# Ternary feed-forward stages of an eight-batch macaron block: most groups' activations transposed by DMA instead of TensorE

## The chip, the cores and the metric

The kernel runs on one core of one Trainium2 chip. The metric is the device time of the whole program in microseconds (us). The profile calls the engines PE (TensorE matrix multiply), PEld (TensorE weight load, which overlaps PE), DVE (VectorE), ACT (ScalarE), POOL (GpSimd) and SP (SyncE, which here issues DMAs).

## The reference

`x` holds 8 x 1024 tokens of width 256. Six sublayers are applied one after the other, each with a residual add and a layernorm in front. They are an FP4-quantized feed-forward, a decaying linear attention, the FP4 feed-forward again, a ternary feed-forward, a memory attention, and the ternary feed-forward again. The ternary feed-forward, the only sublayer that the change touches, is this:

```python
def _L1_ffn_ref(x, W1, b1, W2, b2):
    def _ternary(w):
        scale = jnp.maximum(jnp.mean(jnp.abs(w)), 1e-08)
        w_t = jnp.clip(jnp.round(w / scale), -1.0, 1.0)
        return w + jax.lax.stop_gradient(w_t - w)
    h = jnp.einsum('bsd,fd->bsf', x, _ternary(W1)) + b1
    h = jax.nn.gelu(h, approximate=False)
    return jnp.einsum('bsf,df->bsd', h, _ternary(W2)) + b2
...
x = x + 0.5 * _L1_ffn_ref(_layernorm(x, axis=-1), ...)
```

Its width is 256 in, 1024 hidden, 256 out. The weights are -1, 0 or 1.

## The kernel before

The 8192 tokens stay in SBUF for the whole program as 16 tiles `X[g]` (NG = 16), each [128 partitions, G = 4, D = 256] in float32, that is 512 tokens (TG). A tile is called a group. `ffn_ternary` is called twice, for the fourth sublayer (`ffn_ternary(False, "memory")`) and the sixth (`ffn_ternary(True)`). Below, "the first" and "the second ternary stage" mean these two.

In a ternary stage a group goes through four steps.

- **norm(g)** (L1155): four DVE instructions write the normalized group, tokens in the partitions, into `xn`. `xn_pool` has one buffer.
- **norm_turn(g)** (L1174 to L1179): the matmuls need the feature in the partitions, so PE transposes 2 x 4 blocks of 128x128 against an identity into two PSUM tiles `pt` of one bank each (pool `ps_t`, two buffers). The float32 value is then carried as a sum of two float32r parts: ACT copies `pt` to `xh` (the high part), and DVE writes `xl = pt - xh` (the rest).
- **hidden(g)** (L1193 to L1204): for each of NF = 8 slices of the hidden width, four matmuls of 512 columns (`xh` and `xl`, two halves of the features) fill a PSUM tile `ph` (pool `ps_h`, four buffers). ACT applies Gelu with the bias and writes `hf` in SBUF (L1201; pool `f1_t`, four buffers), copies it to the high part `hh` (L1202), and DVE writes `hl = hf - hh` (L1204).
- **down(g)** (L1220, L1228): for each of the four token tiles, 16 matmuls of 256 columns fill `po` (two banks), and DVE adds half of it to `X[g]`. In the second stage SP then writes the group to HBM.

The loop runs `norm_turn(g)`, `hidden(g-1)` and `down(g-2)` in its round g. Between the slices of `hidden` the entries of a list `between` are called, one for each slice: `norm(g+1)`, `ln.advance(g)` (the layernorm statistics of later groups, DVE, L235 and L236, and the small instructions that turn them into factors, L248 to L264) and, in the last rounds of the first stage, the statistics of the next stage. The last four slices add the output bias to `X` on DVE (`biased`, L1165).

`PLANS["ternary"]` says in what blocks of groups the statistics are taken, (2, 2, 4, 4, 4), and by which round each group's have to be there, `g - 1`. `statistics` spreads the work over the rounds between.

Within an engine the instructions run in the order in which the tile scheduler put them. In these stages the order is not written out by hand (`loose`): the scheduler takes them by priority, roughly the program's order, and puts ready work into gaps. All PSUM (8 banks) is in use: 2 for `pt`, 4 for `ph`, 2 for `po`.

The same program already transposes by DMA in the FP4 stages: SP issues `dma_start_transpose` of a [128, 768] bf16 tile `gd` into `gt` (L912) and of a [128, 512] one into `gtx` (L1084).

Of the kernel before, what the change touches and what calls it, by code (L numbers as in the profile page):

```python
# [9 lines left out]
F32 = mybir.dt.float32  # L10
F32R = mybir.dt.float32r
BF16 = mybir.dt.bfloat16
I32 = mybir.dt.int32
AF = mybir.ActivationFunctionType
ALU = mybir.AluOpType
AX = mybir.AxisListType
PSUM = bass.MemoryType.PSUM

P = 128
D = 256  # L20
# [3 lines left out]
G = 4  # L24
TG = G * P
# [14 lines left out]
def macaron_kernel(  # L40
# [25 lines left out]
    nc = tc.nc  # L66
    NB, S, _ = x.shape
    NG = NB * S // TG
# [21 lines left out]
    xn_pool = ctx.enter_context(tc.tile_pool(name="xn_pool", bufs=1))  # L90
# [39 lines left out]
    for g in range(NG):  # L130
        xg = xpool.tile([P, G, D], F32, name=f"x_{g}")
        X.append(xg)
        if g == 0:
# [4 lines left out]
                out=A0.lng[:, H : H + 2], in_=gamma_rep.rearrange("(m p) -> p m", p=P)  # L138
# [11 lines left out]
    b1c = w_l1.tile([P, NF], F32, name="b1c")  # L150
# [11 lines left out]
    for m in range(NM):  # L162
        nc.sync.dma_start(
            out=mem_d[:, :, m, :],
            in_=memories[m].rearrange("h d e -> (h d) e").rearrange("(c p) e -> p c e", p=P),
        )
        nc.sync.dma_start(
            out=nrm_d[:, :, m],
# [99 lines left out]
    def statistics(sizes, dues):  # L268
# [81 lines left out]
        "fp4": ((3, 1, 2, 4, 4, 2), [0 if g < 3 else G * (g - 2) + 2 for g in range(NG)]),  # L350

        "decay": ((2, 2, 4, 4, 4), [max(0, G * g - 5) for g in range(NG)]),
        "ternary": ((2, 2, 4, 4, 4), [max(0, g - 1) for g in range(NG)]),

        "memory": (
            (GB + 3, 3, 4, NG), [max(0, G * (g - GB) - 4) for g in range(NG)]
# [4 lines left out]
    def begin(kind, left):  # L361

        if kind not in begun:
            ln = statistics(*PLANS[kind])
            begun[kind] = [ln, list(ln.first)]
        ln, shares = begun[kind]
        for _ in range(-(-len(shares) // left)):
            shares.pop(0)()
        if left == 1:
            xn = xn_pool.tile([P, G, D], F32, tag="xn", name="xn")  # L370
            ln.normalize(xn, 0)
            begun[kind] = (ln, xn)
# [26 lines left out]
    def transpose_group(src, dst, psum, tag, both_act=False, pin=lambda ins: ins):  # L399

        for k in range(2):
            pt = psum.tile([P, TG], F32, tag=tag, name="pt")
            for j in range(G):
                pin(
                    nc.tensor.transpose(
                        pt[:, j * P : (j + 1) * P], src[:, j, k * P : (k + 1) * P], ident
                    )
                )
            if k == 0 or both_act:
                nc.scalar.copy(dst[:, k, :], pt)  # L410
            else:
                pin(nc.vector.tensor_copy(dst[:, k, :], pt))

    def fp4_first(xn, mg, pool):

# [722 lines left out]
    def ffn_ternary(last, after=None):  # L1138
        with ExitStack() as st:
            lnp = st.enter_context(tc.tile_pool(name="f1_ln", bufs=2))  # L1140
            hp = st.enter_context(tc.tile_pool(name="f1_h", bufs=2))
            tp = st.enter_context(tc.tile_pool(name="f1_t", bufs=4))
            ps_t = st.enter_context(tc.tile_pool(name="f1_pt", bufs=2, space=PSUM))
            ps_h = st.enter_context(tc.tile_pool(name="f1_ph", bufs=4, space=PSUM))
            ps_o = st.enter_context(tc.tile_pool(name="f1_po", bufs=2, space=PSUM))
            xns, xts, hs = {}, {}, {}
            ln, xns[0] = begun.pop("ternary")
            loose.append("ternary")

            def norm(g):  # L1150
                xn = xn_pool.tile([P, G, D], F32, tag="xn", name="xn")
                for j in range(G):
                    n = G * g + j
                    pin(
                        nc.vector.tensor_scalar(  # L1155
                            xn[:, j, :], X[g][:, j, :], ln.mv[:, n, 0:1], ln.lr[:, n : n + 1],
                            ALU.subtract, ALU.mult,
                        )
                    )
                xns[g] = xn  # L1160

            def biased(j, g):

# [3 lines left out]
            def norm_turn(g):  # L1167
                xn = xns.pop(g)
                xh = lnp.tile([P, 2, TG], F32R, tag="xh", name="xh")
                xl = lnp.tile([P, 2, TG], F32R, tag="xl", name="xl")  # L1170
                for k in range(2):
                    pt = ps_t.tile([P, TG], F32, tag="pt", name="pt")
                    for j in range(G):
                        nc.tensor.transpose(  # L1174
                            pt[:, j * P : (j + 1) * P], xn[:, j, k * P : (k + 1) * P], ident
                        )
                    nc.scalar.copy(xh[:, k, :], pt)
                    pin(
                        nc.vector.tensor_tensor(  # L1179
                            xl[:, k, :], pt, xh[:, k, :].bitcast(F32), ALU.subtract  # L1180
                        )
                    )
                xts[g] = (xh, xl)

            def hidden(g, between):
                xh, xl = xts.pop(g)
                hh = hp.tile([P, NF, TG], F32R, tag="hh", name="hh")
                hl = hp.tile([P, NF, TG], F32R, tag="hl", name="hl")
                for f in range(NF):
                    ph = ps_h.tile([P, TG], F32, tag="ph", name="ph")  # L1190
                    for k in range(2):
                        for xt in (xh, xl):
                            nc.tensor.matmul(  # L1193
                                ph,
                                lhsT=w1[:, k, f * P : (f + 1) * P],
                                rhs=xt[:, k, :],
                                start=(k == 0 and xt is xh),
                                stop=(k == 1 and xt is xl),
                            )
                    hf = tp.tile([P, TG], F32, tag="hf", name="hf")  # L1200
                    nc.scalar.activation(hf, ph, AF.Gelu, bias=b1c[:, f : f + 1])  # L1201
                    nc.scalar.copy(hh[:, f, :], hf)  # L1202
                    pin(
                        nc.vector.tensor_tensor(  # L1204
                            hl[:, f, :], hf, hh[:, f, :].bitcast(F32), ALU.subtract
                        )
                    )
                    if f < len(between):
                        between[f]()
                    elif f >= NF - G:  # L1210
                        biased(f - NF + G, g)
                hs[g] = (hh, hl)
# [24 lines left out]
            for g in range(NG + 2):  # L1237
                between = []
                if g < NG:
                    norm_turn(g)  # L1240
                    if g + 1 < NG:
                        between.append(lambda: norm(g + 1))
                    between.append(lambda: ln.advance(g))
                    if after and g >= NG - 6:
                        between.append(lambda: begin(after, NG - g))
                if 0 <= g - 1 < NG:
                    hidden(g - 1, between)
                else:
                    for do in between:
                        do()  # L1250
                if 0 <= g - 2 < NG:
                    down(g - 2)
# [853 lines left out]
```

## Time and profile before

| | |
|---|---|
| three runs | 2587.45, 2589.17 (median), 2592.93 us |
| the profiled execution | 2594.43 us, of which the span from first to last instruction is 2592.7 us |
| mean granted TensorE clock | 0.993 |
| first ternary stage, from the first to the last of its instructions on the chain | about 1487 to 1749 us |
| second ternary stage | about 2319 to 2590 us |
| DMA, mean over the span | 51 GB/s; 138048 of 199897 packets are under 512 bytes |

A row of the groups of instructions reads: line, engine, operation, output<-inputs, shape, count | busy us in all, mean ns of one | idle time of the engine just before them and what ended most of it. A row of a stretch reads: start:end, its length, then busy us and number of instructions for PE, PEld, DVE, ACT and POOL, then granted PE clock, share of the DMA engines' time, and GB/s. A row of the chain of waits reads: start us, us, what. That chain is followed back from the last instruction, at each step to what released it.

Busy times of overlapping matmuls add up to more than their pitch: the 32 matmuls of 512 columns of a group have a mean of about 400 ns each and take 7.47 us on the chain.

### The profile page before, as it was taken

Reading aid. Unit: us, or ns where it says so; the run is one execution under the profiler, and the core shown is the slowest. Engines: PE = TensorE matmul, PEld = TensorE weight load, DVE = VectorE, ACT = ScalarE, POOL = GpSimd, SP = SyncE. Lnnn points to the kernel's source line nnn. Section 1 sums busy time; section 2 is a strip of 40 time slices with the busy share of each in tenths; the row PEclk is TensorE's granted clock in tenths of the full one; section 3 lists DMA queues with packets and bytes.
Section 4 is the critical chain, followed back from the end, with each engine's and each line's share of the span. In section 5 each row is a group of like instructions: output and inputs, shape, how many; then the busy total and the mean of one; then the engine's idle time right before and its main releaser. Section 6 shows DMA issues by size and latency. Waiting matters only on the chain.

```text
span 2592.7 us, 52415 instructions
## 1 busy us (share of the span) xinstructions
PE 2506.9 (97%) x20426; PEld 1868.6 (72%) x20426; DVE 2087.8 (81%) x4808; ACT 1235.1 (48%) x2785; POOL 900.9 (35%) x895
## 2 busy tenths in 40 slices
PE   4899999999999999999999999999999999999999
PEld 2577777766666666777777689995677776778998
DVE  7898888758878778988888599647888888879864
ACT  5344444334333333444444276656555555437664
POOL 4565555521101003555555300004555555530000
PEclk9899999999999999999999999999999999999999
DMA  7455556500000002556555300000000000000001
GB/s 218 87 117 115 113 118 116 107 23 18 10 22 14 2 2 48 114 116 115 117 116 113 66 1 1 1 1 1 2 2 2 2 2 2 2 2 26 33 33 41
DMA packets 199897, 132.40 MB, mean 51 GB/s; under 512 B 138048, under 2 KB 174944, under 8 KB 199648
## 3 DMA queue, kind: packets, MB, share of 16 engines
q1 hardware_dynamic: 198704, 127.85, 22.8%
q8 instruction: 161, 2.64, 0.4%
q0 software_dynamic: 240, 0.54, 0.1%
q14 instruction: 88, 0.72, 0.1%
q10 hardware_dynamic: 704, 0.66, 0.1%
HBM read 80.77 MB, written 16.52 MB: 38 GB/s over the span
## 4 chain that ended last, share of the span: by engine, by line
PE 84%; DVE 11%; ACT 2%; issue 1%; DMA 1%; POOL 1%; SPq 0%; DVEq 0%; POOLq 0%; ACTq 0%
PE po L960 11%; PE pu L861 10%; PE pg L861 10%; PE po L1220 9%; PE ph L1193 9%; PE sc L1263 5%; PE py L1347 5%; PE pq L1361 4%; PE pkv L1361 4%; PE po L1361 4%; PE pk L1361 4%; PE py L1329 2%; PE pmo L1786 2%; DVE at L1272 1%; DVE qp L804 1%
## 5 line engine op out<-in xcount | busy, mean ns | idle before, releaser
L960 PE MATMUL po<-wd,ht 128*128 128x256 f32 x1536 | 358.1, 383 | 0.6 <-DVE x L969 0.5
L861 PE MATMUL pu<-wgu,xt 128*128 128x352 f32 x1024 | 349.6, 464 | 8.3 <-DVE h L876 7.9
L861 PE MATMUL pg<-wgu,xt 128*128 128x352 f32 x1024 | 348.8, 463 | 4.4 <-ACT sg L871 4.1
L960 PEld LDWEIGHTS po<-wd,ht 128*128 128x128 f32 x1536 | 294.6, 193 | 62.4 <-issue 2.2
L871 ACT ACTIVATE sg<-pg 128x352 f32<-128x352 f32 x256 | 118.1, 461 | 451.5 <-PE pg L861 422.6
L817 POOL TENSOR_TENSOR h<-h,q_rs 128x704 f32<-128x704 f32 (+1 forms) x128 | 176.2, 1376 | 413.1 <-DVE q_rs L811 413.1
L861 PEld LDWEIGHTS pu<-wgu,xt 128*128 128x128 f32 x1024 | 186.5, 193 | 112.3 <-issue 19.6
L861 PEld LDWEIGHTS pg<-wgu,xt 128*128 128x128 f32 x1024 | 195.0, 191 | 97.8 <-ACT sg L871 9.2
L1220 PE MATMUL po<-w,hl 128*128 128x256 f32 x1024 | 243.7, 280 | 1.4 <-DVE hl L1204 1.2
L1220 PE MATMUL po<-w,hh 128*128 128x256 f32 x1024 | 243.3, 280 | 0.0
L1902 POOL TENSOR_TENSOR mo<-mo 128x256 f32<-128x256 f32 x192 | 164.2, 855 | 196.6 <-DVE mo L1799 188.1
L927 POOL TENSOR_TENSOR ht<-gt,ht 128x768 f32<-128x768 bf16 x124 | 205.7, 1659 | 0.0
L1193 PE MATMUL ph<-xh,w 128*128 128x512 f32 x512 | 204.4, 401 | 1.4 <-ACT hf L1201 0.6
L1193 PE MATMUL ph<-xl,w 128*128 128x512 f32 x512 | 201.8, 395 | 0.0
L1204 DVE TENSOR_TENSOR hl<-hf,hh 128x512 fp32r<-128x512 f32 x256 | 168.3, 684 | 39.4 <-ACT hh L1202 35.9
L1220 PEld LDWEIGHTS po<-w,hl 128*128 128x128 f32 x1024 | 192.1, 188 | 4.5 <-DVE hl L1204 2.5
L1220 PEld LDWEIGHTS po<-w,hh 128*128 128x128 f32 x1024 | 192.1, 188 | 2.6 <-DVE x L1228 0.3
L1201 ACT ACTIVATE hf<-ph,b1c 128x512 f32<-128x512 f32 x256 | 168.0, 695 | 18.5 <-PE ph L1193 16.1
L1272 DVE TENSOR_TENSOR at<-sc,dec 128x512 f32<-128x512 f32 x256 | 158.6, 682 | 11.8 <-PE sc L1263 11.8
L886 DVE SCALAR_TENSOR_TENSOR h<-qp,h 128x704 f32<-128x704 f32 x124 | 110.2, 889 | 69.1 <-ACT qp L821 68.9
L1272 DVE TENSOR_TENSOR at<-sc,tri 128x512 f32<-128x512 f32 x256 | 164.9, 679 | 0.4 <-PE sc L1263 0.4
L1202 ACT CAST hh<-hf 128x512 fp32r<-128x512 f32 x256 | 149.2, 628 | 17.0 <-PE po L1220 15.2
(276 smaller groups left out, 5303.0 us busy)
## 6 DMA issues: line engine op xcount, KB each, us to landing
ht<-sd SPq DMA_DIRECT2D x124, 384.0 KB
xt<-sd SPq DMA_DIRECT2D x56, 256.0 KB
sd<-sct SPq DMA_DIRECT2D x124, 64.0 KB
x<-in_x SPq DMA_DIRECT2D x15, 512.0 KB
out<-x SPq DMA_DIRECT2D x15, 512.0 KB
t_raw<-in_w_t SPq DMA_DIRECT2D x16, 256.0 KB
gt<-gd SPq DMA_TRANSPOSE x124
gtx<-xn SPq DMA_TRANSPOSE x56
```

Source lines behind the costliest of these rows:

```text
L817: pin(mul.tensor_tensor(vb, vb, rs[:, :, None].to_broadcast([P, nb, 16]), ALU.mult))
L861: nc.tensor.matmul(ps, lhsT=xts[g][:, 2 * j + k, :], rhs=wgu[:, k, (2 * q + of_up) * NHALF : (2 * q + of_up + 1) * NHALF], start=(k == 0), ...
L927: nc.gpsimd.tensor_tensor(wide.rearrange("p c t -> p (c t)"), grid.rearrange("p c t -> p (c t)"), wide.rearrange("p c t -> p (c t)"), ALU. ...
L960: nc.tensor.matmul(po, lhsT=ht[:kn, c, :], rhs=wd[:kn, c, :], start=(c == 0), stop=(c == NC - 1),)
L1193: nc.tensor.matmul(ph, lhsT=w1[:, k, f * P : (f + 1) * P], rhs=xt[:, k, :], start=(k == 0 and xt is xh), stop=(k == 1 and xt is xl),)
L1201: nc.scalar.activation(hf, ph, AF.Gelu, bias=b1c[:, f : f + 1])
L1202: nc.scalar.copy(hh[:, f, :], hf)
L1204: nc.vector.tensor_tensor(hl[:, f, :], hf, hh[:, f, :].bitcast(F32), ALU.subtract)
L1220: nc.tensor.matmul(po, lhsT=ht[:, f, j * P : (j + 1) * P], rhs=w2[:, f, :], start=(f == 0 and ht is hh), stop=(f == NF - 1 and ht is hl),)
L1272: nc.vector.tensor_tensor(at, sc.rearrange("p m (e t) -> p (m e) t", e=2), weight, ALU.mult)
L1361: nc.tensor.matmul(dst, lhsT=lhsT, rhs=rhs, start=n == 0, stop=n == len(parts) - 1)
L1902: summed = nc.gpsimd.tensor_tensor(mo[:, :, :, 0, :], mo[:, :, :, 0, :], mo[:, :, :, m, :], ALU.add)
```

## The change

Groups 0 to 2 of each ternary stage are transposed by PE as before. For groups 3 to 15 (`by_dma`):

- `norm` writes `xn` into a pool of its own (one buffer), two rounds ahead instead of one. `planes_turned` lets POOL take the float32 words apart into two planes of 16-bit halves (two copies of 1024 elements a partition) and SP transposes both planes, [128, 2048] of 16 bits, in one DMA (two buffers of `turned`).
- `norm_turn` lets POOL join the halves again (`planes_joined`: four copies of 512 elements a partition) into `xf` (one buffer). A function `split` does the rest, and is put at the end of `between`: one ACT copy of 1024 elements to `xh`, and `xl = xf - xh` on POOL instead of DVE.

For all groups, Gelu writes over its input `ph` in PSUM instead of `hf` in SBUF. `hh` and `hl` are then read from `ph`, whose bank is free only after `hl`. `ps_t` and the pool of `hf` are gone. `ps_h` has six buffers instead of four and gives the `pt` of groups 0 to 2 as well. The plan of the statistics has due times one round earlier and smaller first blocks.

```diff
-        "ternary": ((2, 2, 4, 4, 4), [max(0, g - 1) for g in range(NG)]),
+        "ternary": (
+            (2, 2, 2, 2, 4, 4), [0 if g < 2 else 1 if g == 2 else g - 2 for g in range(NG)]
+        ),
...
+    def planes_turned(xn, pool):
+        words = xn.rearrange("p t d -> p (t d)").bitcast(U16).rearrange("p (n b) -> p n b", b=2)
+        apart = pool.tile([P, 2, G * D], U16, tag="apart", name="apart")
+        for b in range(2):
+            nc.gpsimd.tensor_copy(apart[:, b, :], words[:, :, b])
+        turned = pool.tile([P, 2, 2 * G, P], U16, tag="turned", name="turned")
+        nc.sync.dma_start_transpose(
+            out=turned.rearrange("p b n t -> p (b n) t"),
+            in_=apart.rearrange("p b n -> p (b n)"),
+        )
+        return turned
+
+    def planes_joined(turned, dst):
+        words = dst.rearrange("p k t -> p (k t)").bitcast(U16)
+        words = words.rearrange("p (k j t b) -> p b k j t", k=2, j=G, b=2)
+        for b in range(2):
+            for k in range(2):
+                nc.gpsimd.tensor_copy(
+                    words[:, b, k],
+                    turned[:, b].rearrange("p (j k) t -> p k j t", k=2)[:, k],
+                )
...
-            tp = st.enter_context(tc.tile_pool(name="f1_t", bufs=4))
-            ps_t = st.enter_context(tc.tile_pool(name="f1_pt", bufs=2, space=PSUM))
-            ps_h = st.enter_context(tc.tile_pool(name="f1_ph", bufs=4, space=PSUM))
+            gp = st.enter_context(tc.tile_pool(name="f1_g", bufs=2))
+            ps_h = st.enter_context(tc.tile_pool(name="f1_ph", bufs=6, space=PSUM))
...
+            by_dma = lambda g: g > 2
...
-                xn = xn_pool.tile([P, G, D], F32, tag="xn", name="xn")
+                if by_dma(g):
+                    xn = gp.tile([P, G, D], F32, tag="xn", name="xn", bufs=1)
+                else:
+                    xn = xn_pool.tile([P, G, D], F32, tag="xn", name="xn")
...
-                xns[g] = xn
+                xns[g] = planes_turned(xn, gp) if by_dma(g) else xn
...
+                xts[g] = (xh, xl)
+                if by_dma(g):
+                    xf = gp.tile([P, 2, TG], F32, tag="xf", name="xf", bufs=1)
+                    planes_joined(xn, xf)
+
+                    def split():
+                        nc.scalar.copy(xh, xf)
+                        nc.gpsimd.tensor_tensor(xl, xf, xh.bitcast(F32), ALU.subtract)
+
+                    return split
                 for k in range(2):
-                    pt = ps_t.tile([P, TG], F32, tag="pt", name="pt")
+                    pt = ps_h.tile([P, TG], F32, tag="ph", name="pt")
...
-                    hf = tp.tile([P, TG], F32, tag="hf", name="hf")
-                    nc.scalar.activation(hf, ph, AF.Gelu, bias=b1c[:, f : f + 1])
-                    nc.scalar.copy(hh[:, f, :], hf)
+                    nc.scalar.activation(ph, ph, AF.Gelu, bias=b1c[:, f : f + 1])
+                    nc.scalar.copy(hh[:, f, :], ph)
                     pin(
                         nc.vector.tensor_tensor(
-                            hl[:, f, :], hf, hh[:, f, :].bitcast(F32), ALU.subtract
+                            hl[:, f, :], ph, hh[:, f, :].bitcast(F32), ALU.subtract
                         )
                     )
...
-                    norm_turn(g)
-                    if g + 1 < NG:
-                        between.append(lambda: norm(g + 1))
+                    split = norm_turn(g)
+                    for m in (g + 1, g + 2):
+                        if m < NG and by_dma(m) == (m == g + 2):
+                            between.append(lambda m=m: norm(m))
                     between.append(lambda: ln.advance(g))
                     if after and g >= NG - 6:
                         between.append(lambda: begin(after, NG - g))
+                    if split:
+                        between.append(split)
```

More of the change, by code (lines that the diff above doesn't have):

```diff
@@ L13 @@
 I32 = mybir.dt.int32
+U16 = mybir.dt.uint16
 AF = mybir.ActivationFunctionType
@@ L1182, in norm_turn @@
                     )
-                xts[g] = (xh, xl)
             def hidden(g, between):
```

## The prediction, made before the changed kernel was run

> **What bounds the kernel now.** I read the page's busy times first, then the chain of waits in the ternary stages, then those stages in stretches.
>
> ```profile
> PE 2506.9 (97%) x20426; PEld 1868.6 (72%) x20426; DVE 2087.8 (81%) x4808; ACT 1235.1 (48%) x2785; POOL 900.9 (35%) x895
> ```
>
> PE is busy almost throughout. The chain of the first ternary stage shows whether a group's period is PE work alone:
>
> ```profile
> 1646.55 0.87 PE pt L1174 x8
> 1647.42 7.47 PE ph L1193 x32
> 1654.89 7.54 PE po L1220 x64
> 1662.43 0.87 PE pt L1174 x8
> ```
>
> It is. A group takes 1662.43 - 1646.55 = 15.88 us: 0.87 for the eight transposes, 7.47 for `hidden`, 7.54 for `down`, and no wait. The 13 groups from 1515 us on look so, as do 13 in the second stage (from 2356 us). Earlier rounds differ, see below. Next, what the other engines have left (columns: PE, PEld, DVE, ACT, POOL, clock, DMA share, GB/s):
>
> ```profile
> 1500.00:1516.00 16.00, 14.41 (x82) 11.92 (x82) 16.00 (x57) 13.02 (x24) 0.00 (x0) 1.00 0.00 2
> 1568.00:1584.00 16.00, 16.00 (x107) 14.47 (x106) 15.94 (x56) 10.35 (x20) 0.00 (x0) 1.00 0.01 2
> 1648.00:1664.00 16.00, 16.00 (x106) 14.52 (x105) 10.84 (x23) 10.33 (x19) 0.00 (x0) 1.00 0.00 1
> ```
>
> POOL and DMA are idle here. DVE is full until about 1600 us because statistics are taken ahead of need, then busy 10.84 of 16. Only at 1500 to 1516 does PE fall short while DVE is full: there the chain runs over DVE (1491.5 to 1506.7 us).
>
> **What goes.** Per DMA group: eight transposes on PE, two copies on ACT, two subtractions on DVE.
>
> ```profile
> L1201 ACT ACTIVATE hf<-ph,b1c 128x512 f32<-128x512 f32 x256 | 168.0, 695 | 18.5 <-PE ph L1193 16.1
> ...
> L1202 ACT CAST hh<-hf 128x512 fp32r<-128x512 f32 x256 | 149.2, 628 | 17.0 <-PE po L1220 15.2
> ...
> L1179 DVE TENSOR_TENSOR xl<-pt,xh 128x512 fp32r<-128x512 f32 x64 | 41.2, 680 | 1.5 <-ACT xh L1177 1.5
> ```
>
> The mean of a transpose (L1174) is 278 ns, but they overlap: the chain pays 0.87 us for eight, not 2.2. With PE as the bound, 13 groups x 2 stages x 0.87 = **-22.6 us**. DVE loses 2 x 0.68 = 1.36 us a group, which is off the path. A group then takes 7.47 + 7.54 = 15.01 us of PE, and everything else must fit into that.
>
> **What comes, engine by engine.**
>
> POOL, per group: two copies of 1024, four of 512, one subtraction of 1024. No row shows a 16-bit strided copy. The rows nearest, and the far ones:
>
> ```profile
> L1902 POOL TENSOR_TENSOR mo<-mo 128x256 f32<-128x256 f32 x192 | 164.2, 855 | 196.6 <-DVE mo L1799 188.1
> ...
> L1680 POOL TENSOR_SCALAR rt<-rt 96x128 f32<-96x128 f32 x64 | 41.5, 648 | 20.6 <-ACT rt L1674 17.6
> ...
> L1486 POOL TENSOR_TENSOR x<-x,ob 128x1024 f32<-128x1024 f32 x16 | 38.2, 2385 | 341.2 <-ACT xn L317 303.8 <-DVE w L721 22.1 <-DVE t_raw L717 15.3
> ...
> L386 POOL TENSOR_TENSOR xn<-xn,q_rs 128x1024 f32<-128x1024 f32 x2 | 3.9, 1930 | 5.7 <-DVE q_rs L385 5.7
> ...
> L475 POOL CAST df<-ii 128x128 f32<-128x128 int32 x1 | 0.3, 289 | 0.0
> ...
> L484 POOL CAST sf<-ii 128x1 f32<-128x1 int32 x1 | 0.2, 187 | 0.0
> ```
>
> The two CAST rows, one input as in the new copies, give (289 - 187)/127 = 0.80 ns an element over 187 ns: 1.01 us for 1024, 0.60 for 512. With the subtraction at 2.39 (L1486) that is 2.02 + 2.40 + 2.39 = 6.8 us a group. Upper ends: L1902 at 855/256 = 3.34 ns gives 4096 x 3.34 + 2.39 = 16.1 us; L1680 at 648/128 = 5.06 gives 23.1. I take 6.8, since the CAST rows are the same kind of instruction: POOL is under half full, cost nothing. The cover ends at 15.01 us, or (15.01 - 2.39)/4096 = 3.1 ns an element.
>
> DMA, per group: 16 blocks of 128x128. The chain and a stretch in the FP4 stage show 4 blocks (`gtx`) among other transfers, and 6 (`gt`) nearly alone:
>
> ```profile
> 1435.73 4.81 DMA gtx<-xn
> ```
>
> ```profile
> 1426.00:1427.40 1.40, 1.40 (x8) 1.17 (x7) 1.33 (x4) 0.00 (x0) 0.01 (x1) 1.00 1.02 141
> ```
>
> That stretch holds the packets of one `gt`: 196 KB in 1.4 us. So 512 KB takes 3.7 us plus about 1.2 to issue; scaling 4.81 by four instead gives 19.2. I take 5 to 6. SP queues nothing in the first stage but the transposes; in the second, the writes of `out`, ready a round's end later, so neither waits long for the other. Latency: `norm(g+2)` early in round g, joined by round g+2, over 20 us to spare.
>
> ACT: the `xh` copy of 1024 is estimated at 1.05 us (L1202's slope over 512, doubled, less one start), instead of 2 x 0.59. Gelu into PSUM: ACT copies into PSUM of 512 take 621 ns (`mgx`, L821) against 624 within SBUF (L1202), and `hh` from PSUM is like `xh` from `pt`, 587. So 8 x (0.69 + 0.59) + 1.05 = 11.3 of 15.01, nothing.
>
> The new waits: `xh` on ACT waits for POOL's joins; behind it are Gelu and so PE's `ph`. POOL can join group g as soon as `xl` of g-1 is done, a round early, so the wait is empty at 6.8 us. `norm(g+2)` on DVE waits for POOL to have taken group g+1 apart; behind it are the `hl`. That was a round ago.
>
> PSUM: slices in flight between PE and `hl` fall from 8 (four `ph`, four `hf`) to 6. In steady rounds, slice 7 starts 6.5 us into `hidden` and needs `hl` of slice 1, which before was done at 4.8: 1.7 us spare.
>
> **Where I charge something:** the first rounds. At 1503.5 us PE has done ten slices and DVE three `hl`: seven in flight. Six buffers, two of which hold `pt` of group 2, cut that by one to three slices of 0.93 us. Also `norm(3)`, 4 x 0.41 = 1.6 us of DVE, comes a round earlier into rounds where DVE is full. Bounds: 0 (the scheduler puts `hl` first) to 1.6 + 2.8 = 4.4 us a stage, in the far case with nothing regained. I take **3 us a stage, +6**. The extra block of statistics (12 small DVE instructions, pitch about 0.08 us) is in this.
>
> **Sum:** -22.6 + 6 = -16.6 us. The profiled execution, 2594.43 (span 2592.7), would become 2577.8. It ran 5.3 us above the median; the terms are differences of PE time, so the median becomes 2589.17 - 16.6 = **2572.6 us**. Without the charge it is 2566.6; with all of it 2575.4.
>
> DVE beside POOL: L1956 (DVE, two SBUF inputs, in a stage where POOL works) ranges from 241 to 816 ns, up to 0.575 us more. Here the four bias adds a group (L1165) have two SBUF inputs; the new `hl` reads PSUM for one. 4 x 0.575 = 2.3 us fits DVE's spare time in steady rounds (10.84 - 1.36 = 9.5 of 15.01): nothing.
>
> **Rules that speak against it.** The page "VectorE: DVE Perf Modes" of the Trainium skill, section The three transpose paths, gives 1309 ns for a 128x128 block by DMA and 390 on TensorE, and sends 128x128 transposes to TensorE where PSUM will do. By it, 16 blocks would be an estimated 20.9 us a group, over the period, and the change (20.9 - 15.88) x 26 = 131 us slower; the stretch above, six blocks in 1.4 us, contradicts reading it as a rate. The page "GPSIMD Engine Reference" of the same skill, section 4.1 Engine selection, advises against POOL for two-input elementwise work, about half VectorE's speed; the one such instruction a group, 2.39 us by L1486, still fits under the period.
>
> **Rivals.**
> 1. *POOL becomes the bound (slower, 14%).* Mechanism: strided 16-bit copies run at the far rows' rates; `xl` then arrives late for `hidden`. It loses time against before from (15.88 - 2.39)/4096 = 3.3 ns an element on. At L1902's 3.34: (16.1 - 15.88) x 26 = +6, with the start's +6 near 2600; at L1680's 5.06: (23.1 - 15.88) x 26 = +188, 2777. For: no row of a 16-bit strided copy. Against: 0.80 ns for one-input rows.
> 2. *DMA becomes the bound (slower, 3%):* 19.2 us a group, (19.2 - 15.88) x 26 = +86, 2675. Against: the stretch above.
> 3. *Only part is gained (14%):* in the DVE-full rounds up to 1600 us (and to 2425 in the second stage) late `hl` hold `ph`, and PE stops for about 1 us a group in six groups a stage: +12, 2584.6. Against: the 1.7 us spare.
> 4. *Nothing changes (5%):* PE waits elsewhere for what it saves, 2589. Against: a chain of PE alone.
>
> The forecast has 64%, between 2563 (no charge, and DVE's relief helping the start) and 2579. 0.2%, about what a measurement here can tell from no change, is 5.2 us: below 2584 is faster. Rival 3 straddles that, two thirds above faster. Faster: 0.64 + 0.10 = 0.74. Same: 0.04 + 0.05 = 0.09. Slower: 0.17. The range, 2562 to 2596, takes in forecast, rivals 3 and 4, and leaves out rivals 1 and 2.
>
> **What would show it.** Right: in the chain `ph` follows `po` with no `pt` from group 3 on, period 15.0; POOL 6 to 8 us a group; `xh` idle on POOL near zero. Wrong: PE idle before `ph` with a releaser POOL (`xl`), DMA (`turned`) or DVE `hl`; copies of 1024 above 3.2 us; a start longer than 5 us over before's.

## The result, and the profile after

The changed kernel takes 2616.09 us (median of 4 runs, 2614.40 to 2617.88), against 2588.31 for the kernel before (4 runs, 2585.21 to 2592.93). The ratio is 1.0106, 95% interval 1.0088 to 1.0123: slower by 27.8 us, where 16.6 us of gain were forecast, and outside the range. The profiled executions are nearer to each other (spans 2614.4 and 2592.7, +21.7), since that of before (2594.43 us) ran above all four of its timed runs.

Line numbers are now those of the changed kernel: `ph` L1232, `po` L1258, `hl` L1242, `xn` L1185, bias add L1195, `x<-po` L1266, taking apart L422, joining L436, `xl` L1208. First the page's busy times:

```profile
PE 2495.6 (95%) x20218; PEld 1850.1 (71%) x20218; DVE 2100.8 (80%) x4780; ACT 1222.8 (47%) x2759; POOL 1096.3 (42%) x1077
```

PE has 208 instructions fewer (26 groups x 8 transposes) and was busy 11.3 us less, over a span that is 21.7 longer: the time went into waiting. Where, the chain of waits says. This is a piece of the first ternary stage, early and late (start us, us, what):

```profile
1579.51 1.20 DVE hl L1242 x2
1580.80 0.65 DVE x L1195 x2
1581.44 1.20 DVE hl L1242 x2
1582.64 3.05 DVE xn L1185 x3
1585.69 1.20 DVE hl L1242 x2
...
1651.57 7.54 PE po L1258 x64
1659.10 7.47 PE ph L1232 x32
1666.57 7.54 PE po L1258 x64
1674.11 7.47 PE ph L1232 x32
```

From 1650 us on it is what was forecast: no `pt`, and 15.01 us a group (7.54 + 7.47). Ahead of that, where the chain of before was PE from 1515 us on, it now runs over DVE. One piece stands out: three `xn` in 3.05 us, which at 0.41 each would be 1.2. The same two places in the stretches (start:end, length, busy us and instructions of PE, PEld, DVE, ACT, POOL, granted clock, DMA share, GB/s):

```profile
1575.00:1590.00 15.00, 11.66 (x71) 9.87 (x70) 15.00 (x38) 8.12 (x14) 7.04 (x7) 0.96 0.19 36
1665.00:1680.00 15.00, 15.00 (x97) 13.54 (x96) 6.76 (x12) 9.75 (x18) 5.21 (x5) 1.00 0.18 35
```

In the first stretch DVE is "busy" for all 15 us with 38 instructions, and PE idles 3.3 us. In the second DVE needs 6.76 and PE never waits. POOL, ACT and the DMA engines have time to spare in both. So DVE is the bound of the early rounds, though the change took work off it. The groups of DVE instructions between 1500 and 1650 us, shapes kept apart, show which became dearer:

```profile
L1242 DVE TENSOR_TENSOR hl<-ph,hh 128x512 fp32r<-128x512 f32 x71 | 46.8, 677 | 0.3 <-ACT hh L1240 0.3
L1195 DVE TENSOR_TENSOR x<-x,b2h 128x256 f32<-128x256 f32 x62 | 30.9, 510 | 0.0
L1185 DVE TENSOR_SCALAR xn<-x,ln_mv,ln_r 128x256 f32<-128x256 f32 x56 | 29.1, 569 | 1.1 <-POOL apart L422 1.1
```

and the same in the kernel before, between 1500 and 1600 us:

```profile
L1204 DVE TENSOR_TENSOR hl<-hf,hh 128x512 fp32r<-128x512 f32 x55 | 36.2, 678 | 0.3
...
L1165 DVE TENSOR_TENSOR x<-x,b2h 128x256 f32<-128x256 f32 x34 | 13.5, 413 | 0.0
L1155 DVE TENSOR_SCALAR xn<-x,ln_mv,ln_r 128x256 f32<-128x256 f32 x29 | 10.4, 406 | 0.1
```

`hl` costs what it did; the bias adds went from 413 to 510 ns in the mean and `xn` from 406 to 569. A mean hides the form of such a rise. The query by source line gives minimum, median and maximum: 380, 405 and 2501 ns for `xn`. The typical one is unchanged and a few take over 2 us, so I looked at those in the timeline, with POOL's at the same time:

```profile
1532.44 2.37 DVE L265 SCALAR_TENSOR_TENSOR ln_r<-ln_h,ln_r 128x8 f32<-128x8 f32 x1
...
1549.50 2.82 DVE L1185 TENSOR_SCALAR xn<-x,ln_mv,ln_r 128x256 f32<-128x256 f32 x2
```

```profile
1532.40 2.39 POOL L1208 TENSOR_TENSOR xl<-xf,xh 128x1024 fp32r<-128x1024 f32 x1 [5.36 <-ACT xh L1207]
...
1549.68 2.48 POOL L1208 TENSOR_TENSOR xl<-xf,xh 128x1024 fp32r<-128x1024 f32 x1 [8.65 <-ACT xh L1207]
```

The first is an instruction of eight elements a partition, 0.16 us elsewhere. It began 0.04 us after a POOL instruction of 2.39 us and ended at 1534.81, 0.02 us after it. The two `xn` end at 1552.32, POOL's at 1552.16. The DVE instructions of the two stages that took over 0.1 us longer than their shape elsewhere, 70 in all, each end within 0.3 us of the end of a POOL instruction. They are of two kinds: those with two tensors from SBUF (bias adds, the terms `ln_h` and `ln_r`), and `tensor_scalar` (`xn`, `ln_va`). The profile counts the wait as busy time, so no view of waits names POOL for it. It names the next in line:

```profile
PEld po L1258 <- DVE x L1266: 10.4, 9, 2.3
PEld ph L1232 <- DVE hl L1242: 10.0, 13, 1.7
PE po L1258 <- DVE x L1266: 8.2, 7, 2.1
```

(us in total, times, longest.) `hl` and `x<-po` are not slow; they stand behind a DVE instruction that waits for POOL.

The table has what I worked out from each trace. A stage reaches from the first `ph` matmul to the last `po` matmul. "DVE waiting" is the time of DVE instructions beyond what the same shape takes with POOL idle, summed over a stage, first and second; a stretch in which two wait at once (e6, e7) counts once. Stages and waiting are those of the one profiled execution of each kernel.

| kernel | median us | ratio to before, 95% interval | stages, us | DVE waiting, us | longest |
|---|---|---|---|---|---|
| before | 2588 to 2592 | | 256.8, 257.0 | 0, 0 | |
| after | 2616.09 | 1.0106, 1.0088 to 1.0123 | 265.3, 268.8 | 23.6, 23.3 | 2.2 |
| e1 no turning by DMA | 2596.24 | 1.0025, 1.0016 to 1.0035 | 257.2, 257.2 | 0, 0.1 | |
| e2 order kept | 2619.11 | 1.0109, 1.0094 to 1.0124 | 270.4, 267.8 | 22.4, 20.8 | 2.3 |
| e3 Gelu in SBUF | 2655.60 | 1.0248, 1.0233 to 1.0263 | 287.9, 289.1 | 44.3, 42.7 | 2.1 |
| e4 short POOL pieces | 2605.43 | 1.0054, 1.0038 to 1.0071 | 259.5, 264.0 | 10.9, 12.1 | 0.6 |
| e5 short, order kept | 2599.46 | 1.0034, 1.0020 to 1.0047 | 259.0, 257.8 | 10.0, 7.9 | 0.6 |
| e6 DVE relieved | 2631.01 | 1.0152, 1.0135 to 1.0169 | 273.2, 272.4 | 24.9, 21.5 | 2.7 |
| e7 relieved, short | 2642.16 | 1.0207, 1.0167 to 1.0247 | 286.6, 290.4 | 35.7, 36.5 | 10.3 |
| e8 turning left out | 2576.64 | 0.9942, 0.9928 to 0.9957 | 245.3, 247.1 | 0, 0 | |
| e9 groups 8-15, short | 2599.29 | 1.0031, 1.0019 to 1.0043 | 258.8, 259.4 | 5.8, 5.9 | 0.6 |
| e10 groups 8-15, long | 2603.34 | 1.0049, 1.0034 to 1.0064 | 260.9, 259.6 | 12.2, 10.4 | 2.2 |
| e11 as e1, old plan | 2596.74 | 1.0019, 1.0010 to 1.0029 | 258.5, 258.5 | 0, 0 | |
| e12 groups 6-15, short, order kept | 2589.06 | 0.9992, 0.9982 to 1.0001 | 254.3, 253.4 | 5.4, 5.7 | 0.6 |
| e13 as e12, order from hidden(3) | 2584.65 | 0.9978, 0.9969 to 0.9988 | 251.4, 250.8 | 5.4, 5.6 | 0.6 |
| e14 as e13, long pieces | 2619.62 | 1.0115, 1.0097 to 1.0132 | 269.3, 264.9 | 21.4, 18.8 | 2.2 |
| e15 as e11, order kept | 2601.07 | 1.0039, 1.0025 to 1.0053 | 258.4, 258.8 | 0.2, 0.2 | |
| e16 as e13, the change's plan | 2591.03 | 0.9999, 0.9990 to 1.0009 | 254.7, 254.1 | 6.3, 6.3 | 0.6 |

The kernel before, timed anew beside each four, had medians of 2589.37 (e1 to e4), 2591.81 (e5 to e8), 2590.82 (e9 to e12) and 2590.92 (e13 to e16). The ratios are to those.

### The profile page after: what moved, and what is told of

It reads as the page before. It is cut to its first block, busy times and chain, and to the rows that moved or that the text cites. A ratio compares the mean times of both kernels' runs of the same rounds, so it can differ in the third digit from the quotient of the medians.

```text
span 2614.4 us, 52268 instructions
## 1 busy us (share of the span) xinstructions
PE 2495.6 (95%) x20218; PEld 1850.1 (71%) x20218; DVE 2100.8 (80%) x4780; ACT 1222.8 (47%) x2759; POOL 1096.3 (42%) x1077
## 5 line engine op out<-in xcount | busy, mean ns | idle before, releaser
L1258 PE MATMUL po<-w,hh 128*128 128x256 f32 x1024 | 249.0, 284 | 17.6 <-DVE x L1266 17.4
L888 PEld LDWEIGHTS pu<-wgu,xt 128*128 128x128 f32 x1024 | 185.8, 192 | 111.8 <-issue 18.8
L1239 ACT ACTIVATE ph<-ph,b1c 128x512 f32<-128x512 f32 x256 | 169.6, 693 | 171.8 <-PE ph L1232 166.5
L1258 PE MATMUL po<-w,hl 128*128 128x256 f32 x1024 | 247.8, 283 | 0.0
L1242 DVE TENSOR_TENSOR hl<-ph,hh 128x512 fp32r<-128x512 f32 x256 | 168.5, 682 | 73.5 <-ACT hh L1240 73.2
L1232 PE MATMUL ph<-xh,w 128*128 128x512 f32 x512 | 205.8, 402 | 10.5 <-DVE hl L1242 10.4
L1258 PEld LDWEIGHTS po<-w,hh 128*128 128x128 f32 x1024 | 195.3, 191 | 23.1 <-DVE x L1266 21.6
L1232 PE MATMUL ph<-xl,w 128*128 128x512 f32 x512 | 204.3, 399 | 0.0
L1258 PEld LDWEIGHTS po<-w,hl 128*128 128x128 f32 x1024 | 195.6, 191 | 1.7
L1527 POOL TENSOR_TENSOR x<-x,ob 128x1024 f32<-128x1024 f32 x16 | 38.1, 2383 | 341.2 <-ACT xn L318 319.1
L1313 DVE TENSOR_TENSOR at<-sc,dec 128x512 f32<-128x512 f32 x256 | 158.6, 682 | 11.8 <-PE sc L1304 11.8
```

What stands on the lines that cost most here:

```text
L888: nc.tensor.matmul(ps, lhsT=xts[g][:, 2 * j + k, :], rhs=wgu[:, k, (2 * q + of_up) * NHALF : (2 * q + of_up + 1) * NHALF], start=(k == 0), ...
L1232: nc.tensor.matmul(ph, lhsT=w1[:, k, f * P : (f + 1) * P], rhs=xt[:, k, :], start=(k == 0 and xt is xh), stop=(k == 1 and xt is xl),)
L1239: nc.scalar.activation(ph, ph, AF.Gelu, bias=b1c[:, f : f + 1])
L1242: nc.vector.tensor_tensor(hl[:, f, :], ph, hh[:, f, :].bitcast(F32), ALU.subtract)
L1258: nc.tensor.matmul(po, lhsT=ht[:, f, j * P : (j + 1) * P], rhs=w2[:, f, :], start=(f == 0 and ht is hh), stop=(f == NF - 1 and ht is hl),)
L1313: nc.vector.tensor_tensor(at, sc.rearrange("p m (e t) -> p (m e) t", e=2), weight, ALU.mult)
```

## The experiments

The theory: certain DVE instructions wait until the POOL instruction that is running has ended, and `hl` waits behind them. Its rivals were the reorganized PSUM and plan (no POOL at all), the order of DVE's work alone, too few PSUM buffers, and a rate that two engines share. The quoted expectations give them letters.

**e1: all groups turned by PE; Gelu in PSUM, buffers and plan stay.**

```diff
-            by_dma = lambda g: g > 2
+            by_dma = lambda g: False
```

> The changed kernel with PE transposes for all groups: Gelu in PSUM, six ph banks and the new plan of the statistics stay, POOL and DMA have no part in the stages. Theory A (DVE instructions that read two SBUF operands wait until the running POOL instruction ends; about 25 us of such waiting a stage in the changed kernel): no DVE instruction of these stages is lengthened, xn and the bias add stay at 0.41 us, and the time is that of before within the start's charge, 2585 to 2600. Rival B (six banks held until hl are too few, and the early statistics crowd out hl): PE still waits for hl and for x in the rounds up to 1650 us, and the time is 2605 or more.

2596.24, +6.9 on its before, and no DVE instruction is lengthened, as the theory had it. The stages are as long as before (+0.4 and +0.2), and between them it took 1.6 us more; the rest I could not place in a profile. The runs of e1 show a mean granted clock of 0.993 and those of before beside them 0.995, which would be about 4 us if all of the time went by the clock; but e11, which loses nearly as much, shows 0.994, so this settles nothing. So some 21 of the 27.8 us belong to the turning, and the loss inside the stages (8.5 and 11.8 us in the changed kernel) belongs to it almost altogether.

**e2: the DVE fillers (`xn`, statistics, bias adds) may not pass the `hl` of their slice.**

```diff
-                    pin(
+                    low = pin(
...
-                    if f < len(between):
-                        between[f]()
+                    with tc.issue_after(low.ins):
+                        if f < len(between):
+                            between[f]()
```

> The changed kernel, but on DVE the normalization, the statistics and the bias adds of a slice may not be queued before that slice's hl (an ordering edge on the same engine); POOL's work is unchanged. Theory A with order (the waits hurt because the DVE queue was filled with work far ahead of need, so that every wait delays the hl behind it and nothing is made up): DVE still waits some 20 us a stage for POOL, but spread over the whole stage, where a round has about 2 us to spare; PE waits less, 2566 to 2592. Rival D (the waits cost PE their length wherever they stand): 2608 to 2625, as the changed kernel. Rival B (six banks): no better than 2608.

2619.11: nothing gained, in the range of rival D. `xn` no longer waited at all, but the bias adds did (13.8 us in the first stage) and the `ln_r` (4.4), and the next `hl` stood behind them. The order alone is not the cause.

**e3: Gelu to SBUF and the PSUM pools of before, turning by DMA kept.**

```diff
-                    nc.scalar.activation(ph, ph, AF.Gelu, bias=b1c[:, f : f + 1])
-                    nc.scalar.copy(hh[:, f, :], ph)
+                    hf = tp.tile([P, TG], F32, tag="hf", name="hf")
+                    nc.scalar.activation(hf, ph, AF.Gelu, bias=b1c[:, f : f + 1])
+                    nc.scalar.copy(hh[:, f, :], hf)
```

> The changed kernel, but Gelu writes to SBUF again (four buffers), ph has four banks and pt two of its own, as before; apart has one buffer to make room. DMA and POOL work stay. Theory A: hl now reads two SBUF operands, so that it can wait for POOL as well; DVE waiting rises above 25 us a stage and the time is the changed kernel's or worse, 2612 to 2645. Rival B (depth in PSUM): eight slices in flight take the waits for ph away, 2600 or less.

2655.60, worse than the theory's own range: the buffers of before bring nothing back. (That six are enough for a period of 15.01 us is shown by e8, below.) The edit also gives `apart` one buffer instead of two. The answer by source line for `hl`, here and in the changed kernel (minimum, median, maximum):

```profile
L1245 DVE TENSOR_TENSOR hl<-hf,hh x128: 650/688/2548, 1496.5 to 1764.7; 128x512 fp32r<-128x512 f32 x128
```

```profile
L1242 DVE TENSOR_TENSOR hl<-ph,hh x128: 655/681/694, 1496.9 to 1744.1; 128x512 fp32r<-128x512 f32 x128
```

The same subtraction, with its first tensor in SBUF instead of PSUM, now waits too, up to 2548 ns; from PSUM, none of 128 passes 694. For this subtraction it is the two SBUF operands that make it wait, and Gelu in PSUM is what keeps `hl` clear of POOL.

**e4: every POOL instruction of the turning cut into pieces of 256 elements.**

```diff
-            nc.gpsimd.tensor_copy(apart[:, b, :], words[:, :, b])
+            for n in range(0, G * D, 256):
+                nc.gpsimd.tensor_copy(apart[:, b, n : n + 256], words[:, n : n + 256, b])
```

(the joins and `xl` likewise)

> The changed kernel, with POOL's work cut into pieces of 256 elements (apart 8 instead of 2 instructions a group, joins 8 instead of 4, the subtraction 4 instead of 1). POOL's total rises from 7.9 to an estimated 10 us a group. Theory A (a DVE instruction waits for the end of the one POOL instruction that runs): no DVE instruction is lengthened by more than about 0.8 us (2.1 before), total waiting falls from 25 to 10 to 16 us a stage, and the time falls to 2592 to 2608. Rival E (DVE and POOL share a rate, so that the overlap in time counts, not the length of an instruction): waiting stays at 25 us or rises with POOL's total, 2614 or more.

2605.43, in the theory's range and 10.7 below the changed kernel, although POOL's work for the turning is now 125.7 us in the first stage instead of 98.1. The longest wait fell from 2.2 to 0.6 us and their sum from 23.6 to 10.9. The bias add, in the changed kernel and here:

```profile
L1195 DVE TENSOR_TENSOR x<-x,b2h x64: 385/414/1480, 1488.8 to 1648.1; 128x256 f32<-128x256 f32 x64
```

```profile
L1197 DVE TENSOR_TENSOR x<-x,b2h x64: 383/412/959, 1488.2 to 1641.9; 128x256 f32<-128x256 f32 x64
```

A shared rate would have made more POOL work cost more. Here the wait goes by the length of one POOL instruction.

**e5: e2 and e4 together.**

> Both earlier edits together: POOL's work in pieces of 256 elements, and normalization, statistics and bias adds of a slice queued behind that slice's hl. Theory A2 (what hurts is the length of the single wait that stands in front of an hl in the DVE queue; up to 0.6 us is absorbed if no backlog has built up): waiting of about 10 us a stage as with short pieces alone, but PE keeps running, 2575 to 2595. Rival F (every us of waiting costs PE, whatever its length and place; 11 us a stage cost 16 us with short pieces alone): 2600 to 2612.

2599.46, between the two ranges. The first rounds ran at 16 to 17.5 us, nearly all after them at 15.5 or less.

**e6: DVE relieved; `xn` of DMA groups on ACT, bias adds on POOL. e7: the same with short pieces.**

```diff
+                    if by_dma(g):
+                        nc.scalar.activation(
+                            xn[:, j, :], X[g][:, j, :], AF.Identity, bias=nb[:, j : j + 1],
+                            scale=ln.lr[:, n : n + 1],
+                        )
+                        continue
...
-                pin(nc.vector.tensor_tensor(xj, xj, b2h, ALU.add))
+                nc.gpsimd.tensor_tensor(xj, xj, b2h, ALU.add)
```

> The changed kernel, POOL's transposition work in long pieces as it was, but for the groups transposed by DMA the normalization goes to ACT (four instructions a group with scale and bias, plus one DVE instruction of 4 elements for the bias), and all bias adds to POOL (four pieces of 256 a group). Theory A2: DVE has nearly no instruction left that waits for POOL, only the terms of the statistics; waiting falls from 23 to 6 to 12 us a stage, DVE work by 3.3 us a group, time 2572 to 2595. Rival G (POOL's chain from joins to xl, or ACT, is late for hidden by itself): PE waits for xl, 2605 or more.

> As the run before it in this list, with POOL's transposition work in pieces of 256 elements as well (POOL an estimated 13 us a group). Theory A2: single waits of at most 0.6 us, nearly none in front of an hl; 2568 to 2585. Rival G: POOL near full, xl late, 2600 or more.

2631.01 and 2642.16: the theory missed both; they lie in rival G's ranges, though PE waited for `hl` (21.8 and 31.9 us by its weight loads, first stage), not for `xl`. In e6 most of the instructions that had waited are gone from DVE, and it waits about as long as in the changed kernel: POOL, with the bias adds, is busy 136 us of the first stage instead of 98, and the small terms that stay on DVE wait for it. `xn` on ACT also waits for POOL (38.3 us for `apart`), ahead of Gelu. In e7, whose profiled execution was the longest of its four (2660.71), the waits are of a new size. DVE's and POOL's timeline there:

```profile
1571.09 10.47 DVE L249 TENSOR_SCALAR ln_va<-ln_mv 128x16 f32<-128x16 f32 x1
```

```profile
1569.11 3.19 POOL L438 COPY xf<-turned 128x256 uint16<-128x256 uint16 x8
1572.21 2.46 POOL L423 COPY apart<-xn 128x256 uint16<-128x256 uint16 x7
1574.63 2.81 POOL L1210 TENSOR_TENSOR x<-x,b2h 128x256 f32<-128x256 f32 x4
1577.38 1.42 POOL L423 COPY apart<-xn 128x256 uint16<-128x256 uint16 x4
1578.77 1.40 POOL L1210 TENSOR_TENSOR x<-x,b2h 128x256 f32<-128x256 f32 x2
1580.11 0.73 POOL L423 COPY apart<-xn 128x256 uint16<-128x256 uint16 x2
1580.81 0.71 POOL L1210 TENSOR_TENSOR x<-x,b2h 128x256 f32<-128x256 f32 x1
```

A `tensor_scalar` of 16 elements waited 10.3 us, until POOL's unbroken row of short instructions came to its end at 1581.52. It did not get in between two of them. So short pieces help only while POOL also pauses.

**e8: the turning left out from group 3 on; `hidden` uses group 2's operands again.**

> Leaves out the transposition from group 3 on: no taking apart, no DMA, no joining, no xh and xl; hidden uses those of group 2 for all later groups. Normalization on DVE stays, its result is not read. Shows what PE's time would be if the transposed data came for nothing. If the term -22.6 us is right: before plus the 7 us that Gelu in PSUM and the new plan cost, less 22.6, that is 2570 to 2580, period of a group 15.0 us. If something else holds PE: 2585 or more.

2576.64. Against e1, each by its own before, that is -15.2 - 6.9 = -22.0 us: the term of -22.6 was right. The chain:

```profile
1647.00 7.54 PE po L1263 x64
1654.54 7.47 PE ph L1237 x32
```

It is also the ceiling for this arrangement: turning for nothing would bring 15 us over before. Against its stages the changed kernel lost 20.0 and 21.7 us, where its DVE waited 23.6 and 23.3.

**e9 and e10: only groups 8 to 15 turned by DMA, with short and with long pieces; old plan of the statistics for the first eight.** The idea was that DVE has time to spare there. **e11: e1 with the old plan. e12: groups 6 to 15, short pieces, order kept.**

```diff
-            by_dma = lambda g: g > 2
+            by_dma = lambda g: g > 7
...
-            (2, 2, 2, 2, 4, 4), [0 if g < 2 else 1 if g == 2 else g - 2 for g in range(NG)]
+            (2, 2, 4, 4, 4), [max(0, g - 1) if g < 8 else g - 2 for g in range(NG)]
```

> The short POOL pieces (256 elements), but only groups 8 to 15 are turned by DMA, and the statistics keep the plan of before for the first eight groups. Theory A (the waits cost time only where VectorE is full, up to about group 7; later they go into its spare time): 16 groups x -0.87 = -13.9, plus 0 to 7 us for what the kernel without any DMA turning lost: 2576 to 2585, and a period of 15.01 in rounds of DMA groups. Rival G (a waiting VectorE instruction stands before hl and stops TensorE in any round, full or not; changed kernel over the one without turning: (2616.1 - 2576.6)/26 = 1.5 us a group with long pieces, (2605.4 - 2576.6)/26 = 1.1 with short ones): 16 x (1.1 - 0.87) = +4, 2593 or more.

> As the kernel with only groups 8 to 15 turned by DMA, but with the long POOL pieces of the changed kernel. Theory A: within 4 us of the one with short pieces, 2576 to 2588, since VectorE has room for some 5 us of waiting a group there. Rival G: 16 x (1.5 - 0.87) = +10, 2600 or more.

> No group turned by DMA (as the first experiment, which measured 2596.2), and the statistics by the plan of before: only Gelu in PSUM and the PSUM pools remain of the change. If the plan of the statistics is what cost the first experiment its 7 us: 2587 to 2592. If Gelu in PSUM and the six shared buffers cost it: 2594 to 2598.

> Groups 6 to 15 turned by DMA, short POOL pieces, xn and the bias adds kept behind the hl of their slice. Theory A: 20 groups x -0.87 = -17.4, of which groups 6 and 7 may give back some 2 us each a stage, plus 0 to 7 us: 2573 to 2587. Rival G, by the kernel with both edits and all groups: (2599.5 - 2576.6)/26 = 0.88 a group, no gain left: 2590 to 2597.

e9 and e10 measured 2599.29 and 2603.34, as the rival had it and not as I had it, and e12, which turns more groups, 2589.06, between its two ranges and no different from before. Yet most rounds of e9 did run at 15.01. It lost its time in three rounds, 16.8, 18.1 and 18.8 us between the ends of two groups' `down`, while its counted waiting was only 5.8 us a stage. So something besides the waits costs time. Part of it comes after PE has stood: the granted clock is 0.89 in 1625 to 1640 us, where PE is busy throughout. What PE waited for, the chain says:

```profile
1608.87 3.02 POOL xl L1213 x4
...
1611.94 3.83 POOL xf L438 x8
...
1615.79 4.30 DMA turned<-apart
...
1620.21 2.81 POOL apart L423 x8
...
1623.05 0.73 DVE xn L1187 x2
1623.78 0.61 DVE hl L1250
```

The chain goes over POOL and DMA into `xn`, and `hl` comes after it. The `xn` there belongs to a group needed rounds later. The stretches with the instructions of `xn` alone, 1550 to 1580 us, first e9, then before:

```profile
1550.00:1580.00 30.00, 7.90 (x20) 1.00 0.19 36
```

```profile
1550.00:1580.00 30.00, 3.01 (x8) 1.00 0.00 1
```

Before, `xn` had one buffer that PE's transposes freed, so one group's four were done a round. Now POOL frees it, and the scheduler, which puts ready work into gaps, runs through the groups: 20 in two rounds. (In e13 below, with DVE's order kept, it is 8 again.) It ends at the limit of the buffers, where `xn` waits for `apart` (4.1 us in e9's first stage, 6.3 in e4's) with `hl` queued behind. e11 says that the plan is not what costs e1 its 7 us (2596.74, +5.9): the second of its expectations, Gelu in PSUM and the shared buffers, is left, though its stages too are only 1.5 to 1.7 us longer than before.

**e13: e12 with the order kept only from hidden(3) on. e14: the same with long pieces. e15: e11 with the order kept everywhere. e16: e13 with the change's own plan.**

```diff
-                    with tc.issue_after(low.ins):
+                    with tc.issue_after(low.ins) if g > 2 else ExitStack():
```

> As the kernel with groups 6 to 15 turned by DMA, short pieces and DVE's order kept (2589.1), but the order is kept only from hidden(3) on. There, group 2 was done 66 us into the stage, and 61.8 with the free order and no turning; later rounds took 15.0 to 15.3. Theory I (holding the order costs the start, where VectorE has to work ahead): 2 x -4.2, so 2578 to 2585, faster than the kernel before. Rival H (the work that is not done ahead at the start is missing later, or the reverse: the start only shifts it): 2587 to 2592.

> The same with the long POOL pieces of the changed kernel: are short pieces needed once VectorE's order is kept? By the length of the waits (changed kernel against its short pieces: 10.7 us for 26 groups, so 8 for 20): 2586 to 2594. If the order alone was the rest of the loss: within 3 us of the kernel with short pieces.

> No group turned by DMA, the plan of before (that measured 2596.7), and VectorE's order kept in all rounds: the cost of the order by itself, without any wait for POOL. Theory I: the start loses 4.2 us a stage, 2601 to 2608. Rival J (the start of the kernel with 2589.1 lost its time to waits or to the DMA groups): 2595 to 2599.

> As the first kernel of this call, with the change's own plan of the statistics (smaller first blocks, due a round earlier). Without turning, that plan brought group 2 to its end 1.3 us earlier a stage (60.5 against 61.8), though the whole times were alike (2596.2, 2596.7). If the plan matters: 2575 to 2582; if not, as the first within 2 us; if the earlier statistics fill VectorE while POOL works: 2 to 6 us slower.

e13 measured 2584.65, as expected, faster than the kernel before (-6.3 us, interval of the ratio 0.9969 to 0.9988) and some 34 us better than the changed one, each against its own before. The order in the first rounds costs: without it there, e13's stages are 2.9 and 2.6 us shorter than e12's. e15 is 4.3 us slower than e11, without any work on POOL, but its stages are as long as e11's, so where that price lies is not shown. e14, with long pieces, is 35 us slower than e13 and outside both of its expectations: in e13 the order pays only because the waits are short. e16 is 6.4 us slower than e13, so beside the turning the earlier plan costs as well.

A steady stretch of e13 (engines as above), then its bias adds between 1600 and 1700 us:

```profile
1640.00:1655.00 15.00, 15.00 (x98) 13.51 (x97) 11.01 (x29) 9.88 (x18) 9.24 (x20) 1.00 0.19 36
```

```profile
L1197 DVE TENSOR_TENSOR x<-x,b2h 128x256 f32<-128x256 f32 x25 | 11.4, 455 | 0.0
```

The same stretch of e14, its bias adds, and its chain just after:

```profile
1640.00:1655.00 15.00, 13.86 (x86) 12.03 (x85) 12.09 (x27) 9.89 (x17) 6.65 (x7) 1.00 0.18 36
```

```profile
L1195 DVE TENSOR_TENSOR x<-x,b2h 128x256 f32<-128x256 f32 x25 | 20.0, 798 | 0.0
```

```profile
1650.22 0.60 DVE hl L1242
1650.82 2.15 DVE x L1195
1652.98 0.35 DVE x L1267
1653.37 4.04 PE po L1259 x32
```

In e14 DVE is far from full, and PE still loses over 1 us a round. The order puts a bias add beside `xl` in each round; it takes 2.15 us, `x<-po` waits behind it, and PE stops because both banks of `po` are taken (PE's weight loads waited for `x<-po` 19.2 us in that stage, 3.1 in e13). A wait costs by what stands behind it, not by how busy its engine is.

## Why the prediction was wrong

**Right.** The -22.6 us (e8: -22.0) and the period of 15.01. POOL's work: the groups of the first stage

```profile
L436 POOL COPY xf<-turned 128x512 uint16<-128x512 uint16 x52 | 38.5, 805 | 6.9 <-DMA turned<-apart 6.4
L1208 POOL TENSOR_TENSOR xl<-xf,xh 128x1024 fp32r<-128x1024 f32 x13 | 31.3, 2409 | 85.0 <-ACT xh L1207 85.0
L422 POOL COPY apart<-xn 128x1024 uint16<-128x1024 uint16 x26 | 28.3, 1115 | 52.8 <-DVE xn L1185 44.0 <-DVE ln_s L236 4.4 <-DMA turned<-apart 4.4
```

make (38.5 + 31.3 + 28.3)/13 = 7.5 us a group where 6.8 were taken, and `xl` waits for ACT, not PE for `xl`. Rival 1 did not come about. The DMA was right (a transpose stood 4.30 us on e9's chain, 5 to 6 were taken), and so was the `xh` copy (1.04 us in e9, 1.05 estimated).

**The step that failed** is "DVE beside POOL": 4 x 0.575 = 2.3 us a group that "fits DVE's spare time in steady rounds ...: nothing". Three things in it were wrong. Its size: 0.575 us was read from a stage where the POOL instructions (L1902) mostly take 0.73 us. The wait lasts until the POOL instruction that runs has ended, here up to 2.2 us beside one of 2.39; the row to take was that of the new POOL instruction, not of an old DVE one. Its extent: only the bias adds were counted, but `xn` and the small statistics terms wait as well. Its cover: the spare time was taken from the steady rounds, while the prediction had itself noted that DVE was full until 1600 us. There, 23.6 us of waiting in the first stage stand beside 20.0 us that it lost over e8, and short pieces (e4) brought both down, to 10.9 and 14.2.

The page "SBUF — State Buffer" of the Trainium skill, section "Who interferes with whom", says as much: a VectorE instruction with two SBUF inputs and a GpSimd instruction that reads SBUF take turns, and the later one blocks until the other is through. The 2.37 us of an eight-element instruction beside a 2.39 us one agree with it.

**Rival 3** had half of the mechanism, late `hl` holding `ph` in the DVE-full rounds, with a price of 6 us a stage instead of some 20, and still a gain. It did not say that POOL would make `hl` late, and PE waited at least as long for `x<-po` as for `hl`. The 1.7 us of spare time in PSUM that spoke against it is less than one wait.

**"norm(g+2) ... That was a round ago"** failed too, with a smaller bill. It took the order of the program for that of the engine. The scheduler ran `xn` ahead until it did wait for POOL: only 1.1 us in the changed kernel's first stage, but 6.3 and 9.4 in e4's two.

**The charge of 3 us a stage** for the first rounds came near the +6.9 of e1 as a number, but not as a reason: e1's stages are 0.4 and 0.2 us longer. One reading behind it was off, too: at 1503.5 us DVE had done two `hl`, not three (the third begins at 1505.99), so eight slices were in flight, as many as there were buffers.

**Open:** where the rest of e1's 6.9 us lies. And of the 20.0 us in the first stage, 13.7 are idle time of PE beyond e8's (16.0 against 2.3). The first stage of the changed kernel, and a piece of it:

```profile
1491.40:1756.70 265.30, 249.30 (x1552) 219.23 (x1551) 204.90 (x536) 160.41 (x282) 98.46 (x95) 0.99 0.14 27
1588.80:1592.20 3.40, 3.40 (x18) 3.40 (x18) 3.40 (x13) 0.00 (x0) 3.40 (x5) 0.50 0.00 0
```

In the other 6.3 us PE was busy, 249.3 us where e8 took 243.0 for as many matmuls. The granted clock was 0.50 for 3.4 us from 1588.8 us on, which is worth an estimated 1.7 of them; the rest stays open.

## What to carry to other kernels

Work that is moved to POOL is not free for DVE, however idle POOL is: price it by the longest single POOL instruction, for each DVE instruction with two SBUF tensors or of `tensor_scalar` kind that may meet it, and ask what stands behind that one. Where POOL does not pause, a `tensor_scalar` can wait longer still (e7). Short POOL instructions with pauses and a DVE operand in PSUM are the two cures that the runs showed. And where a change removes the consumer that freed a buffer, ask what paced the producer: once PE no longer freed `xn`, it ran ahead of the work on the path. Short pieces and a kept order for all 13 groups were still slower than before (e5); of the kernels that turn by DMA only e13, which also leaves the first six groups to PE and the first rounds' order free, was faster.

## What the runs showed of the hardware that was not expected

- A DVE instruction of eight elements takes as long as the POOL instruction beside it (2.37 against 0.16 us), and the profile books this as busy time.
- In the changed kernel, instructions with one tensor from PSUM (`hl`, 694 ns at most of 256; `x<-po`, 427) and `bn_stats` (406 ns in the mean between 1500 and 1650 us, 411 before) did not lengthen beside POOL. `tensor_scalar` did, though it reads a single tensor and takes the same 0.41 us for 256 elements as the rest. (In e6 an `x<-po` was recorded at 1.11 us and a `bn_stats` at 1.51; both had begun behind a `tensor_scalar` that was waiting.)
- A `tensor_scalar` can wait through a whole row of POOL instructions (10.3 us in e7).
- A strided 16-bit copy on POOL takes 1.12 us for 1024 elements, 0.81 for 512, and in e4 about 0.44 to 0.52 for 256, so cutting `xl` and the copies into pieces raised POOL's work from 98.1 to 125.7 us in the first stage.
